# Two-layer row attention in one launch: the ends of both layers reordered

## The chip, the cores and the metric

The kernel runs on one core of a Trainium2 chip. The metric is the device time of one execution in microseconds (us), taken as the median of several runs. A profile of one execution stands beside the times. The engines are TensorE (PE in the profile; PEld are its weight loads), VectorE (DVE), ScalarE (ACT), GpSimd (POOL) and SyncE (SP), which issues most of the DMA transfers. Matmuls accumulate in PSUM banks; everything else lies in SBUF.

## The reference

The input x has 128 rows of 256 tokens with 256 channels, in float32. Two layers follow one another, each a group normalisation (32 groups over all rows and tokens) with attention inside each row, added to x:

```python
x = x + L0(gn(x));  x = x + L1(gn(x))

# layer 0: 8 heads of 32, every token sees all 256 of its row
sim = softmax(q k^T * scale) + bias            # bias (head, q, k) from pair_repr
out = (sim v * sigmoid(x gate_proj)) out_proj
# layer 1: 4 heads of 64, token i sees j with |i - j| <= 16
attn = softmax(where(|i - j| <= 16, q k^T / 8, -inf))
out = (attn v) w_out^T + b_out
```

Layer 1's group normalisation needs the mean and the variance over layer 0's whole output: no row of layer 1 can be normalised before layer 0's last row is done.

## The kernel before

**Layout and loops.** Channels lie on the partitions (two halves of 128), the 256 tokens of a row along the free axis. Layer 0 walks the rows one by one (L823), with everything of the next row pipelined into the current one; layer 1 walks them in pairs (L1047) and finishes the outputs of a pair two iterations later. Layer 0's output is added into tiles `o` of two rows (L788) and stored to a scratch tensor `x1`, from which layer 1 loads `yg` tiles of two rows (`load1`).

**Order.** Inside `tc.manual_schedule` the order of each engine is the order in which the program writes its instructions: PE, ACT and DVE in layer 0, and POOL too in layer 1. SP, which issues the loads and stores, is not written out there; its DMAs go out as their data are ready. An instruction waits by semaphore for its operands and for a free buffer of its tile's ring; what stands behind it on the same engine waits with it.

**A row in layer 0.** `scores` makes the products of queries and keys and ACT their exp tiles; `join_tiles` adds pairs of these on DVE (four instructions a row, tile `both`); `sum_heads` turns them into the row sums `zs` on PE, with the products of the bias and the values, `bv`. `divide` (L751) copies z on ACT, forms (1 + e^-g) z and its reciprocal d on DVE. `attend` multiplies the exp tiles by the values on PE (`av`), and three DVE multiplications and additions make `at` = (av + bv z) d. `stretch` runs the projections of a coming pair of rows, with the four output matmuls `po` (L634) of the row before woven into them; `finish` (L780) adds x, and takes the statistics of each two rows by `bn_stats` (L791). `least` (L762) keeps the smallest z of a row, for a test at the very end.

**The boundary.** In the row s = 127, `join_most` (L259) joins the statistics of all rows but the last two, in two shares; an extra turn s = 128 then finishes row 127. `channel_columns` (L274) adds the last statistics, takes the mean over the channels of a group with one small matmul (`ps_m`), the variance with another (`ps_v`), and ACT and DVE make 1/std (`rstd`). Layer 1 begins with four weight tiles `1p` set to 0 on POOL (L865), the normalised rows `1xn` (L883) on DVE, their sums `1ts` on POOL, the values `p1v` (L917) and the query and key products on PE, which are of a kind with seven products whose parts POOL adds up (L592, L593).

**A pair in layer 1.** `scores`, with exp on ACT and the band's mask and sum on POOL; `attend` (values, and row sums by a matmul with ones, into the PSUM tile `avz`, two in the ring); `total` (ACT copies the sums to `1z`, L992, two in the ring); `project` (`1po`); `inverse` (DVE reciprocal, L998); `divide` (`1at`, L1004); `least` (`zmin`, L1010). `finish` (L1012) adds bias and x to `1po` in one DVE instruction per half row (`ot`, L1023), turns 32x32 blocks (L1027) into the output tile `1o` (two in the ring), and after the second row of a pair issues four stores, one per strip of 32 partitions (L1033).

**The end.** The smallest and the summed z decide whether all sums were in a safe range (L1076 to L1085): two small matmuls and a cast give a number that PE, SP and the other engines load and branch on; the branch leads to a slow second computation, which these inputs don't take.

## Time and profile before

| | us |
| --- | --- |
| median of 3 runs | 3258.2 (3253.23 to 3259.37) |
| profiled execution, device time | 3257.72 |
| its span on the core | 3256.0 |
| busy: PE / PE weight loads / DVE / ACT / POOL | 3151.5 / 2442.3 / 2678.8 / 2041.1 / 1683.4 |
| layer 0's last 1/std ready (boundary) | 2115.1 |
| first score product of layer 1 | 2129.9 |
| last output store issued | 3250.5 |

The span runs from the first to the last recorded instruction; 1.7 us of the device time lie around it. Busy times overlap between engines. The granted clock of PE was 0.989 of full speed in the mean. A line of an instruction group gives start and duration, engine, source line, operation, output and input tiles, shape and count; in square brackets stands the idle time before the first of them and what ended it. "Issue" there means that the engine waited for nothing that the profile shows.

### The profile page before, as it was taken

How to read it: one execution, taken by the hardware profiler on the slowest of the kernel's cores; microseconds unless marked ns; L12 is line 12 of the kernel's file. 1: busy time of each engine (PE TensorE's matmuls, PEld its weight loads, DVE VectorE, ACT ScalarE, POOL GpSimd, SP SyncE). 2: the span in 40 equal slices, each digit the busy share in tenths (PEclk: the TensorE clock that was granted, in tenths of full speed). 3: DMA queues.
4: the chain of work that ended last, by engine and by line, in shares of the span. 5: the costliest groups of instructions: out<-in, count | busy, mean ns of one | idle time of the engine just before them, and what ended most of it. 6: DMA issues, size and time to landing. Idle time of an engine off the chain costs nothing.

```text
span 3256.0 us, 86773 instructions
## 1 busy us (share of the span) xinstructions
PE 3151.5 (97%) x36937; PEld 2442.3 (75%) x36937; DVE 2678.8 (82%) x3547; ACT 2041.1 (63%) x4306; POOL 1683.4 (52%) x1657
## 2 busy tenths in 40 slices
PE   6799999999999999999999999799999999999997
PEld 4567777777777777777777777588888888888886
DVE  4759999999999999999999999857777777776667
ACT  4566666666666666666666666466666666665663
POOL 3034444444444444444444444287777777776774
PEclk9999999999999999999999999899999999999999
DMA  9931111111111111111111110012222222222221
GB/s 386 414 89 53 53 34 41 35 39 34 40 37 37 34 40 37 37 34 40 40 34 37 37 40 27 21 28 63 57 67 67 67 55 65 67 67 53 61 59 48
DMA packets 346330, 209.36 MB, mean 64 GB/s; under 512 B 273608, under 2 KB 339152, under 8 KB 339664
## 3 DMA queue, kind: packets, MB, share of 16 engines
q1 hardware_dynamic: 345040, 201.37, 21.2%
q8 instruction: 292, 4.78, 0.6%
q0 software_dynamic: 752, 2.36, 0.2%
q14 instruction: 102, 0.84, 0.1%
q10 hardware_dynamic: 144, 0.00, 0.0%
HBM read 136.59 MB, written 67.11 MB: 63 GB/s over the span
## 4 chain that ended last, share of the span: by engine, by line
PE 92%; DMA 3%; DVE 3%; issue 1%; ACT 0%; POOL 0%; SPq 0%; DVEq 0%; ACTq 0%
PE sim L702 8%; PE p1v L917 7%; PE av L729 7%; PE 1po L634 7%; PE po L634 7%; PE bv L729 7%; PE pv L569 6%; PE pq L565 6%; PE p1q L565 5%; PE pk L565 5%; PE p1k L565 5%; PE pg L565 5%; PE zs L743 4%; DMA xs<-in_x_dram 3%; PE 1sim L938 3%; PE 1avz L970 2%
## 5 line engine op out<-in xcount | busy, mean ns | idle before, releaser
L998 DVE RECIPROCAL 1rz<-1z 128x512 f32<-128x512 f32 x128 | 427.8, 3342 | 319.5 <-ACT 1z L992 319.5
L713 ACT ACTIVATE ex<-sim 128x512 f32<-128x512 f32 x1024 | 527.4, 601 | 249.8 <-PE sim L702 249.8
L719 DVE TENSOR_TENSOR both<-ex 128x512 f32<-128x512 f32 x512 | 484.1, 984 | 77.9 <-ACT ex L713 77.9
L759 DVE RECIPROCAL d<-d 128x512 f32<-128x512 f32 x128 | 429.2, 3353 | 4.4
L592 POOL TENSOR_TENSOR v<-v,twovg 128x256 f32<-128x256 f32 x64 | 72.8, 1137 | 551.3 <-ACT twovg L608 551.3
L634 PE MATMUL po<-at,out_sb 128*128 128x256 f32 x1024 | 288.3, 385 | 12.1 <-DVE at L777 12.1
L702 PE MATMUL sim<-q,k 32*128 32x256 f32 x4096 | 295.7, 401 | 1.1 <-ACT ex L713 1.1
L634 PE MATMUL 1po<-1at,w_out_t 128*128 128x256 f32 x1024 | 271.5, 389 | 5.0 <-DVE 1at L1004 3.1
L702 PEld LDWEIGHTS sim<-q,k 32*128 32x128 f32 x4096 | 186.6, 184 | 102.4 <-issue 69.4
L729 PE MATMUL av<-ex,v 128*32 128x256 f32 x4096 | 247.5, 382 | 0.0
L948 POOL TENSOR_TENSOR 1p<-1ex,seen 128x768 f32<-128x768 f32 x128 | 232.7, 1818 | 23.3 <-ACT 1ex L946 23.3
L729 PE MATMUL bv<-bias_sb,v 128*32 128x256 f32 x4096 | 244.5, 379 | 0.0
L917 PEld LDWEIGHTS p1v<-w_in_t,1xn 128*64 128x64 f32 x4096 | 223.6, 137 | 22.0 <-issue 22.0
L917 PE MATMUL p1v<-w_in_t,1xn 128*64 128x128 f32 x4096 | 239.1, 275 | 1.1 <-DVE 1xn L883 1.1
L634 PEld LDWEIGHTS 1po<-1at,w_out_t 128*128 128x128 f32 x1024 | 191.1, 192 | 54.6 <-ACT 1z L992 20.4
L634 PEld LDWEIGHTS po<-at,out_sb 128*128 128x128 f32 x1024 | 187.9, 194 | 34.4 <-issue 7.7
L592 POOL TENSOR_TENSOR q<-q,twoqk 128x256 f32<-128x256 f32 x64 | 47.2, 737 | 298.5 <-ACT twoqk L608 298.5
L729 PEld LDWEIGHTS av<-ex,v 128*32 128x32 f32 x4096 | 120.1, 109 | 108.2 <-issue 42.1
L729 PEld LDWEIGHTS bv<-bias_sb,v 128*32 128x32 f32 x4096 | 133.1, 110 | 87.9
L684 DVE TENSOR_SCALAR xn<-xt,mean,rstd 128x256 f32<-128x256 f32 x256 | 196.8, 808 | 0.0
L593 POOL TENSOR_TENSOR 1q<-1q,mid1q 128x512 f32<-128x512 f32 x64 | 81.6, 1274 | 191.2 <-ACT 1q L589 191.2
L955 POOL TENSOR_TENSOR 1zp<-1p 128x512 f32<-128x512 f32 x128 | 162.6, 1270 | 10.0
(259 smaller groups left out, 7638.3 us busy)
## 6 DMA issues: line engine op xcount, KB each, us to landing
pr<-in_L_conv_pair_repr_dram SPq DMA_DIRECT2D x32, 1024.0 KB, 22.9
x<-o SPq DMA_DIRECT2D x64, 512.0 KB, 2.8
yg<-x SPq DMA_DIRECT2D x64, 512.0 KB, 4.3
out_dram<-1o SPq DMA_DIRECT2D x256, 128.0 KB, 4.3
xg<-in_x_dram SPq DMA_DIRECT2D x252, 128.0 KB, 3.1
xs<-in_x_dram SPq DMA_DIRECT2D x15, 2048.0 KB, 21.8
xs<-in_x_dram SPq DMA_DIRECT2D x2, 1024.0 KB, 17.5
qkv_sb<-in_L_conv_qkv_proj_dram POOLq DMA_DIRECT2D x4, 192.0 KB, 12.2
```

What stands on the lines that cost most here:

```text
L565: nc.tensor.matmul(out, lhsT=weights, rhs=moving, start=first, **flags)
L569: nc.tensor.matmul(out[:, cols], lhsT=moving[:, cols], rhs=weights, start=first and t2 == 0, **flags)
L634: nc.tensor.matmul(ps[:, m, :], lhsT=w[:, kt, m * P : (m + 1) * P], rhs=at[:, kt, :], start=(kt == 0), stop=(kt == 1),)
L684: nc.vector.tensor_scalar(xns[i][:, 2 * r + half, :], xt[:, half, :], mean0[:, half : half + 1], rstd0[:, half : half + 1], op0=ALU.subtra ...
L702: nc.tensor.matmul(sims[j][:, kt, :], lhsT=k[p0 : p0 + D0, 2 * r + half, kt * P : (kt + 1) * P], rhs=q[p0 : p0 + D0, 2 * r + half, :], sta ...
L713: nc.scalar.activation(ex[:, j], sims[j], AF.Exp, scale=1.0 / math.sqrt(D0))
L719: nc.vector.tensor_tensor(both[:, j : j + 2], ex[:, j : j + 2, 0, :], ex[:, j : j + 2, 1, :], ALU.add)
L729: nc.tensor.matmul(to[D0 * j : D0 * (j + 1), half, :], lhsT=v[:, 2 * r + half, c0 : c0 + D0], rhs=weights(4 * half + j, kt), start=(kt == ...
L759: nc.vector.reciprocal(d, d)
L917: nc.tensor.matmul(ps[KB * half : KB * (half + 1), b, :], lhsT=xns[i][:, 2 * r + kt, KB * b : KB * (b + 1)], rhs=w_in_t[:, kt, 2 * C + P * ...
L948: nc.gpsimd.tensor_tensor(p.rearrange("p j (r c) -> p (j r) c", c=WROW)[:, :, 0 : 2 * WSTEP] .rearrange("p r (t c) -> p r t c", c=WSTEP)[: ...
L998: nc.vector.reciprocal(st[s]["rz"], st[s]["z"])
```

## The change

**Statistics.** The class `Most` takes the place of `join_most`; its two joins are written in rows 125 and 126, after `least` and before the projections, instead of both in row 127. The last two rows get a `bn_stats` of their own each, so that three parts instead of one are added in `channel_columns`.

**Layer 0's last rows.** In row 127 the three remaining joins of exp tiles and the least of row 126 come ahead of `attend(126)`. The extra turn is gone: row 127's sums, bias products and values are written ahead of the output products of rows 126 and 127. Between them, and ahead of and behind the two small matmuls of `channel_columns`, stand 4, 5, 2 and 3 filler matmuls (`keep_on`: the identity times `out_sb` into a PSUM bank that nothing reads). The least of row 127 moves behind `rstd`.

**Start of layer 1.** The weight tiles are set to 0 on POOL after the first row sums instead of before.

**End of layer 1.** The rings of `1z` and of `ot` grow from two to four. In the last two iterations (rows 122 to 126) ACT adds the bias, one instruction per half row, and POOL adds x, one per row; DVE keeps this only for row 127. DVE's order there is: reciprocals and divisions of rows 124 to 127, turns of rows 122 and 123, row 127's addition and turns, turns of 126, 124 and 125, then the least of rows 124 to 127. In the other iterations the same instructions are written in the same order on every engine.

```diff
-    def join_most(pool, stats, which):
...
+    class Most:
+
+
+        def __init__(self, pool, stats, late, which):
+            self.stats, self.late = stats, late
+            n = stats.shape[2] - late
+            self.shares = ((0, n // 2), (n // 2, n))
+            self.mv = pool.tile([P, 2, 2, 2], F32, name=f"mv_most{which}")
+
+            self.most = pool.tile([P, 2, 2, 3], F32, name=f"most{which}")
+
+        def join(self, share):
+            n0, n1 = self.shares[share]
             count = (n1 - n0) * 2.0 * R
+            nc.gpsimd.memset(self.most[:, :, share, 0:1], count)
             for half in range(2):
+                nc.vector.bn_aggr(
+                    out=self.mv[:, half, share, :], in_=self.stats[:, half, n0:n1].rearrange("p n s -> p (n s)")
+                )
+            nc.vector.tensor_copy(self.most[:, :, share, 1:2], self.mv[:, :, share, 0:1])
+            nc.vector.tensor_scalar(self.most[:, :, share, 2:3], self.mv[:, :, share, 1:2], count, None, op0=ALU.mult)
+
+    def channel_columns(pool, most, which, wait=lambda n: None):
+
+        stats, late = most.stats, most.late
+        last = pool.tile([P, 2, 2 + 2 * late, 3], F32, name=f"last{which}")
+        nc.vector.tensor_copy(last[:, :, 0:2], most.most)
         nc.vector.tensor_copy(
-            last[:, :, 2:4].rearrange("p h e k -> p h (e k)"), stats[:, :, stats.shape[2] - 1]
+            last[:, :, 2:].rearrange("p h e k -> p h (e k)"),
+            stats[:, :, stats.shape[2] - late :].rearrange("p h n s -> p h (n s)"),
         )
...
+        wait(5)
         ps_m = proj_bank(f"ps_m{which}")
         nc.tensor.matmul(ps_m[:, 0, 0:2], lhsT=within, rhs=means, start=True, stop=True)
...
+        wait(2)
         ps_v = proj_bank(f"ps_v{which}")
         nc.tensor.matmul(ps_v[:, 0, 0:2], lhsT=within, rhs=d, start=True, stop=True)
+        wait(3)
         std = pool.tile([P, 2], F32, name=f"std{which}")
         nc.scalar.activation(std, ps_v[:, 0, 0:2], AF.Sqrt, bias=eps)
...
-        stats1 = st1.tile([P, 2, S // 2, 6], F32, name="stats1")
+
+        stats1 = st1.tile([P, 2, S // 2 + 1, 6], F32, name="stats1")
...
-                if k % 2 == 1:
+                first, part = (k, S // 2 - 1 + k) if s >= S - 2 else (k - 1, s // 2)
+                if first == k or k == 1:
                     for half in range(2):
-                        nc.vector.bn_stats(out=stats1[:, half, s // 2, :], in_=o[:, k - 1 : k + 1, half, :])
+                        nc.vector.bn_stats(out=stats1[:, half, part, :], in_=o[:, first : k + 1, half, :])
...
+                most1 = Most(st1, stats1, 3, 1)
+                for s in range(S):
+                    scores(s, 0)
                     zs = sum_heads(s - 1)
                     join_tiles(s, 0, 0)
                     divide(s - 1, zs)
-                    if s % 2 == 0 and s < S:
+                    if s % 2 == 0:
                         e = res["g", s // 2]
                         nc.scalar.activation(e, e, AF.Exp, scale=-1.0)
-                    if s < S:
+                    z = hd[s - 1, "z"][0] if s > 0 else None
+                    rest = ((0, 2), (1, 0), (1, 2))
+                    if s < S - 1:
                         scores(s, 1)
-                    z = hd[s - 1, "z"][0] if s > 0 else None
-                    attend(s - 1)
-                    for half, j in ((0, 2), (1, 0), (1, 2)):
-                        join_tiles(s, half, j)
-                    least(s - 1, z)
-                    if s == 4:
-                        for weights in quarters1.values():
-                            weights.sum()
+                        attend(s - 1)
+                        for half, j in rest:
+                            join_tiles(s, half, j)
+                        least(s - 1, z)
+                        if s == 4:
+                            for weights in quarters1.values():
+                                weights.sum()
+                        if s >= S - 3:
+                            most1.join(s - S + 3)
+                        stretch(("qk", "vg")[s % 2], s // 2 + 1, s - 1)
+                        normal(s + 4)
+                        if s % 2 == 1:
+                            sum_rows((s + 3) // 2)
+                        finish(s - 1)
+                    else:
+
+                        scores(s, 1)
+                        for half, j in rest:
+                            join_tiles(s, half, j)
+                        least(s - 1, z)
+                        attend(s - 1)
+                load1(0)
+                load1(1)
+                warm = proj_bank("warm")
+
+                def keep_on(n):
+
+                    for _ in range(n):
+                        nc.tensor.matmul(warm[:, 0, :], lhsT=ident, rhs=out_sb[:, 0, :], start=True, stop=True)
+
+                divide(S - 1, sum_heads(S - 1))
+                last_z = hd[S - 1, "z"][0]
+                attend(S - 1)
+                for s in (S - 2, S - 1):
                     if s == S - 1:
-                        most1 = join_most(st1, stats1, 1)
-                        load1(0)
-                        load1(1)
-                    stretch(("qk", "vg")[s % 2], s // 2 + 1, s - 1)
-                    normal(s + 4)
-                    if s % 2 == 1:
-                        sum_rows((s + 3) // 2)
-                    finish(s - 1)
-            mean1, rstd1 = channel_columns(st1, most1, stats1, 1)
+                        keep_on(4)
+                    for _ in one_by_one(out_sb, st[s]["at"], f"po{s}", lambda ps: st[s].update(po=ps)):
+                        pass
+                    finish(s)
+                mean1, rstd1 = channel_columns(st1, most1, 1, keep_on)
+                least(S - 1, last_z)
...
-            for p in weights:
-                nc.gpsimd.memset(p, 0.0)
...
-                z = att.tile([P, 2, R], F32, tag="z", name=f"1z{s}")
+                z = att.tile([P, 2, R], F32, tag="z", name=f"1z{s}", bufs=4)
...
-            def finish(s):
...
+            def add(s, by_vector):
+
                 if s < 0:
                     return
+                po, y = st[s]["po"], ygs[s // XG][:, s % XG]
+                ot = row.tile([P, 2, R], F32, tag="ot", name=f"1ot{s}")
+                st[s]["ot"] = ot
+                for half in range(2):
+                    b = bo_v[:, half : half + 1]
+                    if by_vector:
+                        nc.vector.scalar_tensor_tensor(
+                            ot[:, half, :], po[:, half, :], b, y[:, half, :], op0=ALU.add, op1=ALU.add
+                        )
+                        turn(s, half)
+                    else:
+                        nc.scalar.activation(ot[:, half, :], po[:, half, :], AF.Identity, bias=b)
+                if not by_vector:
+                    nc.gpsimd.tensor_tensor(ot, ot, y, ALU.add)
+
+            def turn(s, half):
+                if s // 2 not in outs:
                     o = big1.tile([P, 2, 2, R], F32, tag="o", name=f"1o{s}")
                     outs[s // 2] = o.rearrange("p s h q -> p (s h q)").rearrange("p (n c) -> p n c", c=C // A)
+                k = s % 2
+                nc.vector.transpose(
+                    out=outs[s // 2][:, k * (R // B) : (k + 1) * (R // B), half * B : (half + 1) * B],
+                    in_=st[s]["ot"][:, half, :].rearrange("p (b t) -> p b t", t=B),
+                )
+
+            def store(s):
+
+                if s >= 0:
+                    o = outs.pop(s // 2)
                     for a in range(A):
                         nc.sync.dma_start(out=in_strips(out[0], s - 1, 2, a), in_=o[strip(a)])
+
+            def finish(s):
+                add(s, True)
 
             load1(0)
             with tc.manual_schedule(engines={
                 mybir.EngineType.PE, mybir.EngineType.Activation, mybir.EngineType.DVE, mybir.EngineType.Pool
             }):
                 normal(0, False)
+                for p in weights:
+                    nc.gpsimd.memset(p, 0.0)
                 values(0)
                 values(1)
                 normal(1, False)
                 nc.vector.scalar_tensor_tensor(shift1, mean1, -1.0, rstd1, op0=ALU.mult, op1=ALU.mult)
                 stretch(0, iter(()))
-                for s in range(0, S + 4, 2):
+                for s in range(0, S + 2, 2):
                     if s < S:
                         scores(s)
                         scores(s + 1)
-                    one, two = (s - 2, s - 1) if s <= S else (-1, -1)
-                    attend(one)
-                    attend(two)
-                    total(one)
-                    total(two)
+                    attend(s - 2)
+                    attend(s - 1)
+                    total(s - 2)
+                    total(s - 1)
                     for _ in project(s - 4):
                         pass
-                    inverse(one)
-                    finish(s - 4)
-                    divide(one)
-                    inverse(two)
-                    divide(two)
-                    least(one)
-                    least(two)
-                    stretch(s // 2 + 1, project(s - 3))
-                    finish(s - 3)
-                    normal(s // 2 + 2, True)
-                    values(s + 2)
-                    values(s + 3)
+                    inverse(s - 2)
+                    if s < S - 2:
+                        finish(s - 4)
+                    divide(s - 2)
+                    inverse(s - 1)
+                    divide(s - 1)
+                    if s < S - 2:
+                        least(s - 2)
+                        least(s - 1)
+                        stretch(s // 2 + 1, project(s - 3))
+                        finish(s - 3)
+                        store(s - 3)
+                        normal(s // 2 + 2, True)
+                        values(s + 2)
+                        values(s + 3)
+                    else:
+
+                        for _ in project(s - 3):
+                            pass
+                        add(s - 4, False)
+                        add(s - 3, False)
+                for s in (S - 2, S - 1):
+                    for _ in project(s):
+                        pass
+                add(S - 2, False)
+
+                def turn_row(s):
+                    for half in range(2):
+                        turn(s, half)
+                    if s % 2 == 1:
+                        store(s)
+
+                for s in (S - 6, S - 5):
+                    turn_row(s)
+                finish(S - 1)
+                for s in (S - 2, S - 4, S - 3):
+                    turn_row(s)
+                store(S - 1)
+                for s in range(S - 4, S):
+                    least(s)
 
```

## Prediction

> **What bounds the kernel.** I read the page first, then the chain of waits, then windows and timelines of the two ends, last layer 1 pair by pair.
>
> ```profile
> PE 3151.5 (97%) x36937; PEld 2442.3 (75%) x36937; DVE 2678.8 (82%) x3547; ACT 2041.1 (63%) x4306; POOL 1683.4 (52%) x1657
> ...
> q8 instruction: 292, 4.78, 0.6%
> ...
> PE 92%; DMA 3%; DVE 3%; issue 1%; ACT 0%; POOL 0%; SPq 0%; DVEq 0%; ACTq 0%
> ```
>
> TensorE (PE) bounds both layers: 92% of the chain. So only the places where it stands or runs slowly can pay: the boundary of the layers (2090 to 2120 us), the end (3220 to 3256), and whatever else stops it. First the boundary, by windows (columns: length, then busy time and instructions of PE, weight loads, VectorE (DVE), ScalarE (ACT), GpSimd (POOL), granted clock, DMA share, GB/s):
>
> ```profile
> 2090.00:2095.00 5.00, 3.68 (x12) 2.68 (x16) 4.97 (x8) 0.00 (x0) 0.00 (x0) 0.66 0.00 0
> ...
> 2100.00:2105.00 5.00, 0.33 (x1) 0.33 (x2) 4.86 (x5) 0.00 (x0) 0.00 (x0) 0.64 0.00 0
> 2105.00:2110.00 5.00, 3.42 (x8) 2.17 (x7) 1.72 (x4) 0.00 (x0) 0.71 (x1) 0.68 0.00 0
> ...
> 2115.00:2120.00 5.00, 4.29 (x54) 4.32 (x56) 4.96 (x10) 0.59 (x1) 3.63 (x5) 0.65 0.01 3
> ```
>
> DVE is full and PE waits for it; then PE works at two thirds of its clock. DVE's order there (start, duration):
>
> ```profile
> 2097.87 0.69 DVE L788 TENSOR_TENSOR o<-po,xt 128x512 f32<-128x512 f32 x1 [0.20 <-PE bv L729]
> 2098.48 0.68 DVE L758 SCALAR_TENSOR_TENSOR d<-g,z 128x512 f32<-128x512 f32 x1
> ...
> 2099.20 3.35 DVE L759 RECIPROCAL d<-d 128x512 f32<-128x512 f32 x1
> ...
> 2108.45 0.69 DVE L788 TENSOR_TENSOR o<-po,xt 128x512 f32<-128x512 f32 x1 [3.24 <-PE po L634]
> 2109.18 1.29 DVE L791 BATCH_NORM_STATS2 stats<-o 128x6 f32<-128x512 f32 x2
> 2110.50 0.98 DVE L278 COPY last<-stats 128x12 f32<-128x12 f32 x1
> ...
> 2111.83 0.72 DVE L285 COPY means<-mv 128x2 f32<-128x2 f32 x1
> ```
>
> Row 127's denominator d starts only at 2098.48, behind row 126's output and two joins of the statistics (2093.49 to 2097.5). Everything after it hangs on it, up to the first normalised row, 1xn, at 2115.16.
>
> **Boundary, step by step.** In after, DVE goes from row 126's reciprocal (2085.75 to 2089.02, unchanged) to row 127's three remaining joins of exp tiles (1.81 as now) to 2090.83, the least of z (0.59), then three multiplications for at 126: 2092.88. d 127 starts at 2093.49, the reciprocal at 2094.21 (now 2099.20: 5.0 earlier), at 127 is there at 2099.63 instead of 2104.6. On PE, av 127 now precedes po 126, which runs at about 2096 to 2097.4; four fillers (0.43 each at full clock) end by 2099.3, ahead of at 127, so they delay nothing. po 127 takes 1.99 as at 3242.00 instead of 3.75: o at 2101.7, against 2108.45, 6.75 earlier. Statistics of one row take 0.75 (estimate from 0.28 for 128x128 and 1.29 for two of 128x512) instead of 1.29; the copies 0.17 instead of 0.98 and 0.72, which ran beside the POOL memset (4.31) that now comes later: 1.3 together. So ps_m, the matmul of the means, stands at 2104.1 (now 2112.60), and with unchanged steps rstd ends at 2106.3 (now 2115.1), then the moved least of row 127 costs 0.6: 1xn at 2106.9, **8.3 earlier**. The two early joins (2.0 each) lie in rows 125 and 126, where DVE idles 1.4 a row before o; at most 0.6 is left over, which PE's queued products cover; uncovered it would be 4.0.
>
> After 1xn, PE does the values product in 5.05 (3.71 in a steady pair) because its clock is down; the fillers at ps_m and ps_v should keep it up, worth 0.85 to 1.0 here. But the memset, now between row sums 0 and 1 on POOL, pushes POOL's first 1q addition to 12.2 after 1xn against 12.76 now; that caps this at 0.55. Together 8.8; the clock changes on a grid of 3.41 us (2091.16, 2094.6, 2101.4, 2108.2), and one unlucky phase costs 0.6. The five fillers before ps_m need 2.15 of the 2.4 us in which PE would wait there, the next two 0.86 of 0.84, the last three 1.3 of 1.7: hidden. At half clock a filler takes 0.94 (po 127 today: 3.75 for eight matmuls of this size, two a filler), and these ten would be 4.4 late. I take **8.6**, bounds 6 to 9.5.
>
> The clock row weighed against a rule: windows with 1.37 us of PE work in 3.41 were followed by half clock, those with 1.95 or more were not. The Trainium skill, "TensorE: Matmul & The Clock Gate", section "What's actually happening", has the same free-running window but says that it falls after an idle window; by that rule alone the half-busy windows here would have stayed fast and the fillers would be worth nothing; the trace says otherwise.
>
> **End, step by step.**
>
> ```profile
> ACT 1z L992 <- DVE zmin L1010: 9.2, 1, 9.2
> ...
> 3243.05 0.47 DVE L1023 SCALAR_TENSOR_TENSOR 1ot<-1po,bo_v,yg 128x256 f32<-128x256 f32 x1
> ...
> 3248.35 0.12 DVE L1085 CAST n_fine<-ps_f 1x1 int32<-1x1 f32 x1
> ```
>
> The first line (waits, 3216 to 3256): ScalarE's 1z waits 9.2 us for a z buffer, since the ring holds two; four buffers end that. DVE is full from 3219.89 to 3248.43: four reciprocals (3.35), four divisions (0.6), 12 additions (0.44, with one transpose 0.84 a pair), four least. Of these additions 10 go to ACT (0.47 each) and POOL (1.27 a row), which are idle there (no busy time in 3236 to 3246). The reciprocals now run back to back: at 127 at 3235.6 (now 3241.25), turns of 122 and 123 to 3237.7, row 127 to 3240.1, turn 126 to 3240.8. Turn 124 waits for its ring of two: store 123 is issued at 3237.75, and today's store of that pair landed some 3.7 after its last transpose, so 3241.5. Its turns end at 3243.2, four least (2.45), low and fine: cast at 3246.6, **1.75** earlier. The last output stores: 7 issues of 0.49 behind the last transpose instead of 4, from 3243.25 to 3246.7, against 3250.47 now: **3.7** earlier. Behind the cast come PE's and SP's branches (PE 4.4 us, to 3253.5, SP to 3253.8); which of the two chains binds is not shown. Bounds 1.75 and 3.7; I take **2.4**, nearer to the cast, whose branch ends last in two engines.
>
> **What the diff does not name: instruction fetch.** Every pair of rows of layer 1 should take 17.05 us. These do not (pairs 48, 49, 50, windows):
>
> ```profile
> 2941.40:2958.45 17.05, 17.05 (x254) 14.84 (x252) 12.27 (x14) 11.09 (x25) 12.86 (x13) 1.00 0.24 63
> 2958.45:2979.74 21.29, 19.05 (x254) 16.14 (x252) 12.54 (x14) 11.08 (x25) 12.84 (x13) 0.92 0.22 55
> 2979.74:2998.60 18.86, 17.28 (x254) 14.89 (x252) 12.54 (x14) 11.09 (x25) 12.84 (x13) 1.00 0.23 57
> ```
>
> and PE's waits from 2950 to 3200 are "issue", that is, for nothing seen:
>
> ```profile
> PE 1avz L970 <- issue: 7.7, 5, 2.2
> PE 1avz L980 <- issue: 4.1, 4, 1.5
> ```
>
> Pairs 49 to 58 take 21.29, 18.86, 18.31, 18.57, 19.08, 18.76, 18.27, 18.54, 18.69, 18.21; with the next three **19.2 us** too much. Queue q8's 292 packets carry 16.4 KB each, and 2 x 36937 PE instructions are 253 a packet: one block of about 256. A pair issues 508 PE instructions, so the block's edge moves 4 instructions on in every pair. The gaps lie at the pair's instruction 252, 256, 260 and so on to 288 in pairs 49 to 58: at the edge. In these pairs the trace shows q8's packet landing at 2 to 3 us into the pair, inside the burst of input load and output stores (some 2600 packets in 0 to 5 us), and the gap ends when the next one lands. Elsewhere the edge is reached later and nothing waits.
>
> After issues 57 more PE instructions ahead of layer 1 (14 fillers of two loads and two matmuls, and one wait). The edge moves from 4p+56 to 4p-1 in pair p, so the zone 252 to 300 is left by pairs 49 to 61 and entered by pairs 0 to 12; pair 63 ends at 251. The first pairs have no output burst yet; from pair 3 (edge 267) on I put down what pairs 53 to 61 pay: 2.03, 1.71, 1.22, 1.49, 1.64, 1.16, 0.23, 0.16, 0.77, sum 10.4. The worst, 4.24 and 1.8 for pairs 49 and 50, fall away. 19.2 - 10.4 = **8.8** gained, 8 with some loss at the first stall (pair 49 lost 2 us to a clock drop). Bounds: 0 (the same sum) and 18 (only the last three remain).
>
> A rule speaks against this term: the Trainium skill, "Runtime: NRT & Kernel Launch", section "Instruction fetch mechanics", has blocks of 256 instructions on the sequencer's own queue, but calls the crossing mostly hidden. The 13.6 us of gaps at the edge (0.6 to 2.2 each) do not agree. By the rule this term would be nothing and the time some 3247.
>
> **Sum.** The profiled run took 3257.7 with a span of 3256.0; the median 3258.2 lies 0.5 above. 3257.7 - 8.6 - 2.4 - 8 = 3238.7; I say **3239**.
>
> **Rivals.**
> - *The fetch stalls come out equal* (the zone is swept whole at the start, bursts there being as long): only the reorder counts, 3258 - 11 = 3247. For it: the zone is 13 pairs wide and pairs 0 to 12 cross it. Against: pairs 0 to 2 have no stores. 0.17.
> - *The stalls nearly vanish* (early packets land sooner, as they do at 3.0 to 3.5 in pairs 3 to 12 now, with nothing waiting): 3258 - 11 - 18 = 3229. 0.12.
> - *The reorder gives half* (turn 124's ring, late clock, joins not hidden): -5.5 and -8: 3244. 0.08.
> - *The fillers are the new wait*: if the clock is down when they start, the four hold po 127 back by 3.5, po 127 takes 1.8 more, the other ten 4.4: 9.7 against the 8.6 gained, 3258 + 1.1 - 2.4 - 8 = 3249. 0.04.
> - *The other side: each early stall drops the clock.* Pair 49 paid 4.24 because its gap of 2.24 left too little work in a clock window. If pairs 3 to 12 all pay that, 42.4 instead of 19.2: 3258 - 11 + 23.2 = 3270. It turns slower once the mean of ten stalls is above 3.0 ((19.2 + 11) / 10). Against: nine of ten gaps were 0.7 to 1.7 and dropped nothing. 0.04.
>
> **How the numbers follow.** Forecast 0.55 (3231 to 3246). 0.2%, 6.5 us, is about what a measurement can tell; faster means under 3251.7. The forecast, the vanishing, the half and nearly all of the equal case are faster: 0.91; same 0.05 (the tails of the fillers and of the equal case), slower 0.04. The range 3229 to 3250 takes in the bounds of the fetch term and leaves out the last rival, the tail of the fillers and half of the vanishing case.
>
> **What would show it.** Boundary: reciprocal 127 at 5.0, o at 6.7, 1xn at 8.3 before today's, clock 1.0 throughout, first 1sim 8 to 9 earlier. Fetch: pairs 49 to 61 at 17.05, gaps in pairs 3 to 12 at instructions 267 to 303. End: counted from reciprocal 124, at 127 is 5.7 earlier and the cast 1.75; 1z waits for no buffer; DVE waits at turn 124. I am wrong if stalls sit at other instructions than these, if joins delay rows 125 or 126, or if the clock is down in po 127.

## The result, and the profile after

| | before | changed |
| --- | --- | --- |
| median, us | 3258.78 (6 runs, 3253.23 to 3261.42) | 3237.71 (6 runs, 3235.92 to 3240.07) |
| ratio, with its 95% interval | | 0.9939 (0.9929 to 0.995) |
| profiled execution / span | 3257.72 / 3256.0 | 3237.33 / 3235.6 |
| row 126's reciprocal starts at | 2085.75 | 2085.84 |
| from there to the first 1xn | 29.40 | 21.58 |
| to the first scores of layer 1 | 44.16 | 35.57 |
| to pair 2 of layer 1 | 71.20 | 63.90 |
| time above 17.05 a pair, pairs 2 to 62 | 19.4 | 8.0 |
| end of pair 62 to end of span | 39.64 | 37.87 |

The kernel is 0.61% faster. A pair here is two rows of layer 1, counted from its first score product to that of the next. The table splits the 20.4 us between the two spans (3256.0 - 3235.6): 7.3 up to pair 2, 11.4 in the middle of layer 1, 1.8 at the end, and 0.1 lost before the boundary.

The page of the changed kernel, with the lines shown of the old one:

```profile
PE 3152.0 (97%) x36965; PEld 2443.7 (76%) x36965; DVE 2677.0 (83%) x3539; ACT 2045.6 (63%) x4316; POOL 1689.8 (52%) x1662
...
q8 instruction: 293, 4.80, 0.6%
...
PE 92%; DMA 4%; DVE 3%; ACT 0%; issue 0%; POOL 0%; SPq 0%; DVEq 0%; ACTq 0%
```

TensorE (PE) issues 28 matmuls more, the fillers, and works as long as before; VectorE (DVE) has eight instructions less. "Issue" has gone from 1% of the chain to 0%: that is the middle of layer 1. The boundary by windows:

```profile
2090.00:2095.00 5.00, 4.34 (x64) 2.34 (x64) 4.34 (x8) 1.97 (x3) 0.00 (x0) 1.00 0.00 0
...
2100.00:2105.00 5.00, 4.34 (x20) 3.53 (x20) 3.92 (x12) 0.00 (x0) 0.00 (x0) 1.00 0.20 67
2105.00:2110.00 5.00, 4.71 (x49) 3.91 (x50) 3.89 (x12) 0.26 (x1) 1.28 (x2) 1.00 0.12 42
...
2115.00:2120.00 5.00, 3.66 (x15) 2.02 (x13) 1.61 (x2) 3.90 (x10) 4.92 (x7) 1.00 0.00 0
```

The granted clock is 1.00 in every window where it was 0.64 to 0.68, and PE is busy where it stood still (4.34 instead of 0.33 from 2100 to 2105, 2.3 of it with fillers). DVE's order, by start and duration:

```profile
2094.14 0.69 DVE L771 SCALAR_TENSOR_TENSOR d<-g,z 128x512 f32<-128x512 f32 x1 [0.48 <-DVE at L790]
2094.86 3.35 DVE L772 RECIPROCAL d<-d 128x512 f32<-128x512 f32 x1
...
2102.44 0.69 DVE L801 TENSOR_TENSOR o<-po,xt 128x512 f32<-128x512 f32 x1 [0.70 <-PE po L646]
2103.16 0.75 DVE L805 BATCH_NORM_STATS2 stats<-o 128x6 f32<-128x256 f32 x2
...
2103.95 0.18 DVE L286 COPY last<-stats 128x36 f32<-128x36 f32 x1
...
2104.59 0.17 DVE L294 COPY means<-mv 128x2 f32<-128x2 f32 x1
```

Row 127's denominator starts at 2094.14 instead of 2098.48, its output addition waits 0.70 instead of 3.24 for PE, and the two copies that took 0.98 and 0.72 beside the memset take 0.18 and 0.17 without it. Next, two pairs of rows, 3 and 4, and what was the worst one, 49:

```profile
2166.80:2185.60 18.80, 17.41 (x258) 15.04 (x256) 12.54 (x14) 11.09 (x25) 12.85 (x13) 1.00 0.25 62
2185.60:2203.80 18.20, 17.29 (x258) 14.93 (x256) 12.54 (x14) 11.08 (x25) 12.86 (x13) 1.00 0.23 58
2959.10:2976.20 17.10, 17.10 (x258) 14.89 (x256) 12.27 (x14) 11.09 (x25) 12.91 (x13) 1.00 0.24 63
```

The slow pairs are now at the start of layer 1. PE's waits from 2150 to 2300 (line; us, times, longest) are of the old kind:

```profile
PE 1avz L1017 <- issue: 2.6, 3, 1.1
PE 1avz L1007 <- issue: 1.4, 1, 1.4
PE 1po L646 <- issue: 0.9, 2, 0.7
```

The gaps over 0.3 us stand at instructions 268, 272, 276, 284 and 292 of pairs 3, 4, 5, 7 and 9, that is at 4p + 256, one off 4p - 1 + 256. Which of the records that start together is counted first decides by one or two. Counted one way in all traces, by the order of starts, the gap of pair p lies at 4p + 58 in the kernel before and at 4p + 257 here: counted round a block of 256 that is 57 back, as many as the instructions added. From 2950 to 3195 PE has no wait at all.

Last the end, by the chain of what ended last (start, length):

```profile
3220.95 2.73 DMA out_dram<-1o
...
3223.80 1.43 DVE 1o L1073 x4
3225.23 2.36 DVE zmin L1047 x4
...
3228.59 0.15 DVE n_fine L1165
```

The turns of rows 124 and 125 wait for the store of rows 122 and 123, as foreseen, and the four least and the cast follow. This view leaves out what SP does behind the cast; experiment 8 has it.

### The profile page after: what moved, and what is told of

It reads as the page before. It is cut to its first block, busy times and chain, and to the rows that moved or that the text cites. A ratio compares the mean times of both kernels' runs of the same rounds, so it can differ in the third digit from the quotient of the medians.

```text
span 3235.6 us, 86853 instructions
## 1 busy us (share of the span) xinstructions
PE 3152.0 (97%) x36965; PEld 2443.7 (76%) x36965; DVE 2677.0 (83%) x3539; ACT 2045.6 (63%) x4316; POOL 1689.8 (52%) x1662
## 4 chain that ended last, share of the span: by engine, by line
PE 92%; DMA 4%; DVE 3%; ACT 0%; issue 0%; POOL 0%; SPq 0%; DVEq 0%; ACTq 0%
PE sim L715 8%; PE av L742 7%; PE p1v L954 7%; PE 1po L646 7%; PE po L646 7%; PE bv L742 7%; PE pv L581 6%; PE pq L577 6%; PE p1q L577 5%; PE pk L577 5%; PE p1k L577 5%; PE pg L577 5%; PE zs L756 4%; DMA xs<-in_x_dram 3%; PE 1sim L975 3%; PE 1avz L1007 2%
```

## The experiments

All times are medians; the kernel before, run beside each group on the same chip, had 3260.0 (experiments 1 to 4), 3259.1 (5 to 8) and 3259.3 (9 to 12). "Stalls" is the time above 17.05 us in pairs 2 to 62 of the profiled execution.

**1. Only the instruction count** (the old kernel, fillers at the start of layer 0):

```diff
                 mybir.EngineType.PE, mybir.EngineType.Activation, mybir.EngineType.DVE}):
+                early = proj_bank("early")
+                for _ in range(14):
+                    nc.tensor.matmul(early[:, 0, :], lhsT=ident, rhs=qkv_sb[:, 0, 0:R], start=True, stop=True)
```

> The kernel before with nothing changed but 14 filler matmuls at the very start of layer 0, where TensorE waits for the first statistics: 58 more TensorE instructions ahead of layer 1 and no reorder at all. Theory (instruction fetch): the block edge is moved as in the changed kernel, so the stalls leave pairs 49 to 61 (all 17.05 us) and come back in pairs 3 to 11, at instructions 267 to 303 of the pair, with about 8 us in sum instead of 19: 11 us below before, some 3248. Rival (the middle of layer 1 gained through the change of the layer's own code, four z buffers above all): this kernel takes before's time within 0.2% and still stalls in pairs 49 to 61.

Measured: 3257.48, ratio 0.9995 (0.9985 to 1.0004). The time speaks for the rival, the trace doesn't. Pairs 3 and 4, and 49:

```profile
2181.74:2202.59 20.85, 19.08 (x255) 16.21 (x254) 12.54 (x14) 11.09 (x25) 12.82 (x13) 0.92 0.24 55
2202.59:2221.08 18.49, 17.27 (x255) 14.91 (x253) 12.54 (x14) 11.10 (x25) 12.84 (x13) 1.00 0.24 57
2979.30:2996.35 17.05, 17.05 (x258) 14.85 (x256) 12.27 (x14) 11.09 (x25) 12.85 (x13) 1.00 0.24 62
```

The stalls moved to pairs 3 to 11 with nothing else changed, gaps at 266 to 298. But they are 13.2, not 8, and the fillers were not free where I had put them:

```profile
194.19 6.21 PE L817 MATMUL early<-qkv_sb,ident 128*128 128x256 f32 x28
```

PE went on to its first projections only after them: row 126's reciprocal starts 6.1 us later. From there pair 2 comes another 1.6 later (72.81 instead of 71.20), with TensorE at half clock for 20.5 us instead of 17.1 on the way. Against these 7.7 stand 6.2 us gained in the stalls.

**2. The changed kernel without fillers** (`for _ in range(0)` in `keep_on`, the function that writes them).

> The changed kernel without its 14 fillers: layer 1 starts at the same TensorE instruction as in the kernel before. Theory: the stalls are back in pairs 49 to 61 with 19 us (11 more than in the changed kernel), and TensorE's clock is down for parts of the boundary, which costs 0.5 to 2 there: 3238 + 11 + 1.5, some 3250. Rival (four z buffers or other parts of the reorder cleared the stalls): only the boundary loses, 3239 to 3240.

Measured: 3243.01. The stalls are back in pairs 49 to 61, so no z buffer cleared them, but with 14.2 us instead of 19.4, which neither theory had. The boundary without fillers: first 1xn at 22.61 from row 126's reciprocal, first scores at 37.41, pair 2 at 64.17, against 21.58, 35.57 and 63.90 with them.

**3. The changed kernel, its fillers at the start of layer 0** (2 and the edit of 1).

> The changed kernel with its 14 fillers taken from the boundary and put at the very start of layer 0. The block edge stands as in the changed kernel, the boundary runs without fillers. Theory: stalls in pairs 3 to 11 with some 8 us, and the boundary alone shows what the fillers do for the clock: 0.5 to 2 us, time 3238.5 to 3240. Rival (the fillers matter through the clock and not through their number): as the kernel without fillers, some 3250.

Measured: 3243.44. Stalls of 7.9 in pairs 3 to 11, as the theory has it; the time, 3238.5 to 3240 by the theory, misses. As in 1, the fillers at the start (7.00 there) were not free: row 126's reciprocal starts 5.5 later than in 2. And from there pair 2 comes 2.9 later than in 2 (67.06 against 64.17), with TensorE at half clock for 17.1 us instead of 10.2 on the way, though the boundary has the same instructions in both.

**4. Without some output stores:**

```diff
-                    for a in range(A):
-                        nc.sync.dma_start(out=in_strips(out[0], s - 1, 2, a), in_=o[strip(a)])
+                    if s < 90 or s > 122:
+                        for a in range(A):
+                            nc.sync.dma_start(out=in_strips(out[0], s - 1, 2, a), in_=o[strip(a)])
```

> The kernel before without the output stores of rows 90 to 121, which are left unwritten; everything else, the instruction count of TensorE too, stays. Theory (a block's fetch is late because it lies in the burst of the stores and the input load): in pairs 49 to 61 only the load is left, and their excess of 19.2 us falls to 0 to 6: some 3240 to 3246. Rival (a block's edge at these instructions costs by itself, whatever the DMA queues carry): pairs 49 to 58 still take 18.2 to 21.3 and the time stays at before's.

Measured: 3244.27, stalls 6.7 in pairs 49 to 58. PE's waits from 2950 to 3200, to be held against 7.7 (L970) and 4.1 (L980) before; of L980 there are none:

```profile
PE 1avz L970 <- issue: 2.9, 5, 1.4
PE 1po L634 <- issue: 0.4, 1, 0.4
```

The block edge stands where it stood; what the DMA queues carry sets the price. In pair 54 the trace has queue q8's packet at 2.43 us into the pair in the kernel before (0.96 long; PE goes on at 4.77), at 2.02 in experiment 2 (PE goes on at 4.22) and at 1.00 here, with no gap above 0.3. PE resumes 1.2 to 1.6 us after the packet is in. Of the 15.7 us in the time the stalls explain 12.7; for the rest no run was made.

**5 and 6. One end alone.** Experiment 5 has the changed kernel's layer 0 and memset with the old layer 1, experiment 6 the old layer 0 with the changed rings and end of layer 1.

> The changed kernel's layer 0, boundary and later memset, with layer 1's loop and end as before. The block edge stands as in the changed kernel. Theory: the boundary gives its 7.3 us as in the changed kernel and the end gives back 1.8. Stalls in pairs 3 to 12: if the shorter DMA bursts (and with them stalls of 8 instead of 13 us) come with layer 0's part, which makes the statistics tile longer and so moves the tiles behind it, some 8 us and 3240; if they come with layer 1's deeper rings, 13 us and 3245. Rival (the whole gain lies in layer 1's code): above 3250.

> The kernel before with only layer 1's end and its rings as in the changed kernel; no TensorE instruction more ahead of layer 1. Theory: stalls stay in pairs 49 to 61, with 19 us (then the time is 1.8 below before, some 3257) if the bursts stay as in the kernel before, or with 14 us (3252) if the deeper rings are what shortened them. Rival (the four z buffers clear the stalls): 3249 or less.

Measured: 3240.86 and 3255.5. In 5 pair 2 starts at 64.07 from row 126's reciprocal and the stalls are 8.0, pair for pair those of the changed kernel; in 6 they are 20.3 in pairs 49 to 61. So the deep rings do nothing for the stalls; the lower price of one stall comes with layer 0's part.

**9. The addresses.** The statistics tiles are longer in the changed kernel (by 48 and 96 bytes a partition, from their shapes), and what is behind them stands higher in each partition. I took that to be 160 bytes; no trace holds an address. Only a shift by 160:

```diff
         stats1 = st1.tile([P, 2, S // 2, 6], F32, name="stats1")
+        pad = st1.tile([P, 40], F32, name="pad")
+        nc.gpsimd.memset(pad, 0.0)
```

> The kernel before with a tile of 160 bytes a partition put behind the statistics tile (and set once): the tiles that layer 1 loads into and stores from stand at the addresses of the changed kernel, 160 bytes higher, and nothing else differs. Theory (the shorter stalls at the same block edge, 14 instead of 19 to 20 us, come with these addresses): packets of a pair land 0.15 us earlier in the mean, stalls in pairs 49 to 61 of 14 us, 3254. Rival (they come with layer 0's new order or some other part of it): 19 to 20 us and 3259 as in the kernel before.

Measured: 3254.79, ratio 0.9984 (0.9975 to 0.9994), stalls 14.4. PE's waits from 2955 to 3205:

```profile
PE 1avz L972 <- issue: 5.6, 5, 1.7
PE 1avz L982 <- issue: 3.5, 4, 1.3
```

The unplanned half of the gain is found: 160 unused bytes make the old kernel 4.5 us faster, and its stalls are, pair by pair, within 0.3 us of those of experiment 2. The mean start of a pair's data packets, from the start of the pair (those of its first 8 us, average over undisturbed pairs 16 to 45), is 2.53 here, 2.59 to 2.70 in the four kernels with the old addresses, and 2.47 to 2.54 in the other nine, with the new ones.

**7. Stepping over the zone:**

```diff
-                    for _ in range(n):
-                        nc.tensor.matmul(warm[:, 0, :], lhsT=ident, rhs=out_sb[:, 0, :], start=True, stop=True)
+                    for _ in range((n + 1) // 2):
+                        nc.tensor.matmul(
+                            warm.rearrange("p a b -> p (a b)"), lhsT=ident,
+                            rhs=out_sb.rearrange("p a b -> p (a b)"), start=True, stop=True,
+                        )
...
                 ps = proj_bank(f"p1v{s}").rearrange("p a (b c) -> p (a b) c", c=P)
+                for _ in range(9 if s == 104 else 0):
+                    nc.tensor.matmul(
+                        ps[0:KB, 0, 0:2], lhsT=xns[i][:, 2 * r, 0:KB], rhs=w_in_t[:, 0, 2 * C : 2 * C + 2],
+                        start=True, stop=True,
+                    )
```

> The changed kernel with eight fillers of twice the width instead of 14, so that layer 1 starts 33 instructions later than in the kernel before instead of 57, and with nine matmuls of two columns (36 instructions, overwritten at once) in pair 51. Theory: the block edge starts at instruction 23 of a pair, leaves the zone (up to 44) by pair 5, and is set back by 36 before it reaches 252: stalls of 1 us in all instead of 8, the nine matmuls cost 1 to 2.5: 3232 to 3233. Rival (stalls belong to certain pairs or to some number of blocks): they come back in pairs 52 to 62 and the time is 3238 or more.

Measured: 3232.42, stalls 2.0, of which 1.04 is the price of the nine matmuls in pair 51. From 2150 to 3190 one wait is left:

```profile
PE 1po L646 <- issue: 0.4, 1, 0.4
```

Here the theory was used to make a time, 5.3 us below the changed kernel, and gave it.

**8. Least instructions in DVE's waits** (`least(S - 4)` ahead of `finish(S - 1)`, two more ahead of the turns of rows 124 and 125).

> The changed kernel with three of the four last least instructions moved into the waits of VectorE at the end (0.8 for row 127's product, 1.3 for the output ring). Theory (the cast and the branches behind it end the kernel): the cast is 1.8 earlier, the time 3236. Rival (the last seven store issues end it): the cast is earlier and the time stays at 3237.7.

Measured: 3236.86; the single runs (3235.85 to 3239.23) lie among those of the changed kernel (3235.92 to 3240.07). From the end of pair 62 the cast comes 1.25 earlier (29.57 against 30.82), but the last store issue is done 0.9 later (32.71 against 31.78) and the span ends 0.2 later. The theory fell: the cast is not what ends this kernel. SP loads the cast's number only after its last store issue, then branches. The branch stands among SP's waits (before, changed, 8):

```profile
SPq L1087 <- SPq L1087: 2.7, 1, 2.7
...
SPq L1167 <- SPq L1167: 3.2, 1, 3.2
...
SPq L1170 <- SPq L1170: 2.5, 1, 2.5
```

From the end of pair 62, in us:

| | before | changed | 8 | 2 |
| --- | --- | --- | --- | --- |
| cast | 31.97 | 30.82 | 29.57 | 30.83 |
| PE's branch done | 37.17 | 36.43 | 35.23 | 35.82 |
| SP's last store issue done | 34.09 | 31.78 | 32.71 | 31.80 |
| SP's branch, from and to | 34.69, 37.41 | 32.38, 35.59 | 33.30, 35.86 | 32.83, 36.28 |
| end of span | 39.64 | 37.87 | 38.09 | 38.51 |

In all fourteen traces the span ends 2.23 to 2.28 after SP's branch is done, and in between SP's instructions follow one another within 0.12 us until the engines meet for the last time. So the chain through SP's last store issue ends every one of them. The branch itself is longer where the others branch at the same time: 3.2 to 3.5 us in the eight kernels in which SP's starts within 1 us of PE's, 2.6 to 2.9 in the six in which it starts about 2 us or more behind. Why is not shown.

**11. A third output tile**, in the place of a tile of normalised rows that is done:

```diff
+                    if s == S - 4:
+                        o = row.tile([P, 4, R], F32, tag="xn", name=f"1o{s}", bufs=2)
...
-                for s in (S - 6, S - 5):
+                for s in (S - 6, S - 5, S - 4, S - 3):
                     turn_row(s)
                 finish(S - 1)
-                for s in (S - 2, S - 4, S - 3):
-                    turn_row(s)
+                turn_row(S - 2)
```

> The changed kernel with a third output tile for rows 124 and 125 (in the place of the last normalised rows, which are done), so that their turns stand before row 127's addition and wait for no store. Theory, from the runs so far: the span ends 7.0 after the cast or 5.4 after the last store issue, whichever is later. VectorE loses its wait of 1.3 and the idle 0.8: cast 2.0 earlier, last issue some 4 earlier, end 2.0 earlier: 3235.7. Rival (only the stores end it): 4 earlier, 3234.

Measured: 3236.41. DVE has no wait left in this stretch (timeline):

```profile
3219.43 0.69 DVE L1041 TENSOR_TENSOR 1at<-1avz,1rz 128x512 f32<-128x512 f32 x1
3220.04 2.72 DVE L1078 STREAM_TRANSPOSE 1o<-1ot 128x256 f32<-128x256 f32 x8
3222.68 0.44 DVE L1059 SCALAR_TENSOR_TENSOR 1ot<-1po,bo_v,yg 128x256 f32<-128x256 f32 x1
...
3228.46 0.15 DVE L1169 CAST n_fine<-ps_f 1x1 int32<-1x1 f32 x1 [0.37 <-PE ps_f L1167]
```

From the end of pair 62 (3200.0) the cast comes at 28.47, 2.4 earlier than in the changed kernel, the last store issue is done 2.5 earlier and the span ends 2.5 earlier, at 35.4. Both chains moved alike, so this run does not tell them apart. In the median 1.3 of it is seen: this profiled execution had stalls of 9.3 and began layer 0 later, and single runs of one kernel lie 2 to 4 us apart.

**10. A smaller memset:**

```diff
-                    nc.gpsimd.memset(p, 0.0)
+                    parts = p.rearrange("p j (r c) -> p (j r) c", c=WROW)
+                    nc.gpsimd.memset(parts[:, :, WQ:WSTEP], 0.0)
+                    nc.gpsimd.memset(parts[:, :, WSTEP + WQ : WROW], 0.0)
```

> The changed kernel with only those columns of the four weight tiles set to 0 that nothing else writes (448 of 1216 columns each). Theory (GpSimd sets the pace from the first normalised row to pair 2): 4.3 us of memset become about 1.8, the first scores and pair 2 start 2.5 earlier, and the clock drop in pair 0 (1.5) may go with the shorter wait: 3234 to 3235.5. Rival (TensorE's chain sets the pace there): 3237.7 as it is.

Measured: 3237.69, nothing. POOL gets through earlier and then waits itself:

```profile
2117.00 0.72 POOL L604 TENSOR_TENSOR 1q<-1q,two1qk 128x256 f32<-128x256 f32 x1
2119.69 1.26 POOL L605 TENSOR_TENSOR 1q<-1q,mid1q 128x512 f32<-128x512 f32 x1 [1.97 <-ACT 1q L601]
```

The first scores come 0.43 earlier (35.14 from row 126's reciprocal), pair 2 0.64 earlier (63.26); behind the memset ACT's copies of PE's products are next. So the memset's new place costs 0.4 to 0.6, not the 2.5 that I had put down for it, and the median doesn't show that much.

**12. All of 7, 10 and 11 in one kernel.**

> All three together with the moved block edge: wide fillers and nine matmuls in pair 51, only the gaps of the weight tiles set to 0, and the third output tile. If the parts add up: 3237.7 - 5.3 - 2.5 - 2.0 = 3228. If the wait for GpSimd and the clock eat one of them: 3230.

Measured: 3230.69, ratio to the kernel before 0.9905 (0.9888 to 0.9921), the fastest of all; stalls 2.0, cast at 28.47 from the end of pair 62. 10 adds nothing to it, as it did nothing alone.

**The stalls side by side.**

| kernel | instructions added ahead of layer 1 | addresses | pairs | stalls, us |
| --- | --- | --- | --- | --- |
| before / 6 | 0 | old | 49 to 61 | 19.4 / 20.3 |
| 4 (fewer stores) | 0 | old | 49 to 58 | 6.7 |
| 1 | 58 | old | 3 to 11 | 13.2 |
| 2 / 9 | 0 | new | 49 to 61 | 14.2 / 14.4 |
| changed / 5 / 3 | 57 / 57 / 58 | new | 3 to 11 | 8.0 / 8.0 / 7.9 |
| 7 / 12 | 33, and 36 in pair 51 | new | 3, 5 (and 51) | 2.0 / 2.0 |

Moving the edge takes 6.2 off, at old and at new addresses; moving the addresses takes 5.2 off, at either edge. Together that is the 11.4.

## Why the prediction was right, point by point

**Boundary, 8.6 predicted.** The first scores of layer 1 came 8.59 earlier (44.16 - 35.57), the first 1xn 7.82 instead of 8.3. The missing half microsecond is the idle 0.48 ahead of row 127's denominator: `d` has one buffer, and the new order puts its next use right behind `at` 126, which still reads it. I had put the two back to back. The joins in rows 125 and 126 cost nothing: row 126's reciprocal starts 0.09 later. The four fillers ended by 2099.6, ahead of at 127 (2100.3), and po 127 took 1.99. But of the 8.59 only 7.3 are left at pair 2. The clock drop that I priced at 0.6 came later and cost 1.5: behind PE's wait for the first key sums (2.75) pair 0 ran on at half clock. Windows of pair 0, with the clock in the third column from the right:

```profile
2121.00:2124.00 3.00, 2.26 (x64) 1.96 (x64) 0.00 (x0) 0.87 (x2) 2.28 (x3) 0.76 0.03 5
2124.00:2127.00 3.00, 3.00 (x17) 2.42 (x10) 0.00 (x0) 1.46 (x3) 2.92 (x3) 0.67 0.00 0
```

In experiment 8 the same wait, 2.87, fell otherwise: clock 1.00, pair 0 in 12.58 instead of 14.15, and pair 2 at 62.43. So 0.6 was too low a price for an unlucky phase; here it is 1.5, and experiments 1 and 3 lost up to 1.6 and 2.9 so. The bounds of the clock row (1.37 and 1.95 us of work in a window) hold at the old kernel's boundary but are no threshold: near that kernel's start the window from 207.03, with 2.31 us, was followed by half clock, and in experiment 1 that from 2095.50, with 1.46, was not.

**The fillers.** Through the clock they give 1.0 up to 1xn and 1.84 up to the first scores (experiment 2), and 0.27 up to pair 2 in these two executions, since the drop in pair 0 came only with them. Against experiment 3, which has their number but not their place, they give 3.2 up to pair 2 (63.90 against 67.06): what the clock is worth goes by how its windows fall. Of the 5.3 us between the times of 2 and the changed kernel most is their number, since they move the block edge: in the profiled executions the stalls differ by 6.2, the way to pair 2 by 0.3.

**The cap by POOL**, 0.55 beyond 1xn, let 0.77 through: POOL's first addition of `1q` came 11.3 after 1xn, not 12.2. Most of the memset taken away gave another 0.43 and no more, as ACT's copies are next (experiment 10).

**Instruction fetch, 8 predicted, 11.4 measured.** The step holds: stalls left pairs 49 to 61 and came back in pairs 3 to 11, at the instructions named, with 1.7, 1.1, 1.2, 0.7, 1.7, 0.3, 1.0, 0.0 and 0.4 against the 2.03 to 0.16 put down. The term that was mis-sized is the price of one stall, taken from the old kernel's pairs. At the same edge it fell from 13.2 to 7.9 in sum (experiments 1 and 3) because the tiles moved by 160 bytes, which I had not looked at: 10.4 was predicted to stay and 8.0 did; at the old addresses it would have been some 13, a gain of 6. Two errors of opposite sign, then: the first stall after pair 2 was underrated (pair 3 paid 3.8 there, clock drop included), and the addresses were not seen. That the second outweighed the first, and the term came out too small and not too large, is luck.

Two readings in the step were wrong, though the count held. The gap does not end when the next packet lands (6.2 to 8.0 us into pairs 49 to 58) but 1.2 to 1.6 us after the first one has, at 2.8 to 3.9. And it is not that elsewhere the edge is reached later: in pair 48 it stands at 248 and is passed at 2.8 us, a packet lands at 4.85, and nothing waits. What differs is the time to the edge behind it. A pair's first 256 instructions take 2.9 us, the other 252 take 14. In pair 51 the edges stand at about 4 and 260: TensorE is at the second after 2.9 us, but the packet that begins after the first (1.96, in at 2.84) lets it go on only at 4.18. In pair 48 they stand at 248 and 504, 13.9 us apart. That a packet brings the block behind the next edge is worked out from these times and not shown by itself. The burst is needed too: pair 2 of the changed kernel has its edges in the same zone, but no data packet in its first 5 us, and takes 17.05; its packet is in at 1.36.

The rule weighed against this term, from the Trainium skill ("Runtime: NRT & Kernel Launch", "Instruction fetch mechanics"), that crossing a block is mostly hidden, holds for 53 of the pairs 2 to 62 in the changed kernel (17.05 us); in the other eight, where the fetch meets the burst of loads and stores, the trace has 0.3 to 1.7 us each.

**End, 2.4 predicted, 1.8 measured.** At 127 came as worked out (19.4 from the end of pair 62, forecast 19.2). The wait for the store of rows 122 and 123 lasted longer: from the issue to the turn of row 124 4.55, not 3.7. So the cast came 1.15 earlier instead of 1.75 and the last store issue 2.3 instead of 3.7. What the prediction had wrong is which chain binds: it counted SP's branch to the cast and leaned that way, but the branch stands behind SP's last store issue, and that chain ends both kernels (experiment 8). Of its 2.3 us, 0.5 went into a longer branch of SP, 3.2 instead of 2.7. That 2.4, picked between two bounds, came near 1.8 is luck. In experiment 6, at the old addresses, the turn of row 124 came at most 3.9 after the issue and the end gained 2.8. So the shift that helped in the middle may have cost some 1 us here, but that is one execution.

**The sum** came out 1.3 us from the median by luck, because these errors cancelled (boundary 1.3 and end 0.6 too much, fetch 3.4 too little). Of the rivals, the equal stalls are what the old addresses would have come nearer to; the vanishing ones were made by experiment 7; no early stall dropped the clock at the new addresses, while at the old ones one did (pair 3 of experiment 1: 20.85 us, clock 0.92).

## What to carry to other kernels

Where an engine has "issue" waits at a steadily moving place in a repeated iteration, count its instructions against the blocks of its fetch queue: a few instructions more or less ahead of the loop, or one step of a few dozen inside it, move or remove the stalls, and any reorder that changes the count moves them too. So a change in time after a small edit is not to be put down to the edit before the same count and the same tile addresses have been tried without it. How many instructions lie between two edges counts less than how long they take. At the end of a kernel, write down for each engine what stands last on it, branches too, with its distance to the end: here the cast looked like the end, and SP's branch behind its last store issue was. An edit on the other chain shows nothing.

## What the runs showed of the hardware

TensorE waited for instruction packets of 16.4 KB that came late among some 2600 data packets: 0.3 to 2.2 us a time, and it went on 1.2 to 1.6 us after the packet had landed. Moving the tiles behind the statistics by 160 bytes in SBUF brought the data packets of a pair 0.1 us forward in the mean (2.53 instead of 2.64, experiment 9) and took 4.5 us off the kernel before; loads of a pair landed in 4.1 instead of 4.2 to 4.3 us in the median, stores in 4.1 to 4.2 instead of 4.2 to 4.3. Why is not shown, and only this one distance was tried. DVE copies of 128x2 and 128x12 took 0.72 and 0.98 us while POOL set memory, and 0.16 to 0.17 without it. SP's branch at the end took 2.6 to 3.5 us, and longest where PE's began within 1 us of it.
